# Two feed-forward layers on one core: the last activation in two halves, and stores of different batches untied

## The chip, the cores and the metric

The kernel runs on one core of one Trainium2 chip. The metric is device time in microseconds (us). Three runs of the kernel before took 1050.55, 1051.12 and 1052.24 us, median 1051.12 us. In names of engines, PE is TensorE, DVE is VectorE, ACT is ScalarE, POOL is GpSimd and SP is SyncE.

## The reference

The input x has 16 batches of 256 rows of 256 float32 values; cond_8 gives each batch 8 scores. Two layers follow each other, and each adds its result to x.

- Layer 0: each batch takes the one expert of 8 with its largest score. `hidden = silu(x Wup + bup) * (x Wgate + bgate)`, width 512; `x = x + hidden Wdown + bdown`.
- Layer 1: each batch takes its two best experts with weights w (a softmax of the scores, made to sum to 1), and in addition a shared expert that all batches use. Each expert is `(gelu(x Wgate) * (x Wup)) Wdown`, width 1024. The result is `x + sum of w * expert(x) + shared(x)`.

## The kernel before

**Units.** The work is cut into units. A `Pair` takes two batches that use the same expert and multiplies them as 2 x 2 blocks in Winograd's variant of Strassen's scheme, with 7 block products in place of 8 (`STEPS`, `Pair.up`, `Pair.down`). A `Single` takes one batch in the plain way. Layer 0 has 4 pairs and several singles; layer 1 has 12 routed pairs (`pairs`), 8 shared pairs (`shared`, the expert that all batches use) and singles for what is left over. Which batches form a pair is found on the chip, and a few variants ("arms") of the program's later parts are chosen by that.

**A pair's work.** The hidden width is cut into 4 quarters in layer 1 (2 in layer 0). For quarter j, PE does the seven steps `up(j, 0..6)`. For these POOL first makes four sums of the quarter's weights (`sums_q`, which calls `sums_a`: lines 479 to 482, tile s), except in the shared pairs behind the first, which load sums stored earlier. ACT copies PSUM results (line 522, tile cp), and DVE combines them with others into the four blocks C11, C21, C12, C22 of tile c (line 526): C11 after step 1, C22 after step 4, C21 after step 5, C12 after step 6. In layer 1, `act(j)` then takes gelu of the gate half of all four blocks on ACT (line 577, 128x1024) and multiplies by the other half on DVE (line 580, 128x1024) into blocks 0 to 3 of a tile of ring bt. `act_sums(j)` makes the three further sums on DVE (lines 472 to 474). When all quarters are there, `down(0..6)` multiplies with the down weights (line 597, four quarters in one step, so 8 matmul records), whose sums on POOL are `sums_d` (again lines 479 to 482, tile ds). `early` reads a first result out of PSUM (line 619 on ACT, or 612 on DVE in the last unit), and `late` finishes a block into tile ys (lines 626 and 630 on DVE).

**Order.** No scheduler orders the instructions: they are issued as the program is written. A small planner, `Line`, holds a clock: `line.main` runs a PE step and advances it, `line.later(n, f)` runs f once the clock is n further. `when_free(tag, f)` puts f off until a buffer of that ring has been given back (`give`). Engines and DMA queues each work in order, so an instruction that waits holds up all that stands behind it on its engine.

**Stores.** `done` puts a unit's `send` on a list, and the next `quarter` runs it. In layer 1 `send` issues on POOL one accumulating DMA per batch into `out` (line 451), so each batch's own row gains the unit's result. In layer 0 it issues on SP two plain DMAs per batch, to `x1d` (line 453) and to `out` (line 454). The row is an index held in a register, so the framework cannot know that two stores go to different rows: each waits until the one before it into the same tensor has landed. POOL's sums `s` and `ds` stand behind the stores on POOL; weight loads (line 409, 418) stand behind those of layer 0 on SP.

**The last unit**, `shared[-1]`, does not use `done`. It has loaded what `out` holds (`load_z`, line 515), adds it in `early`, and stores each finished quarter of the result from `late` (line 633): batch 0 on SP, batch 1 on ACT. Only here were stores of different batches declared independent, and only within the unit. Its last `act(3)` waits for a buffer of ring bt, which the unit before it, `shared[-2]`, gives back at its own `down(6)`.

Of the kernel before, what the change touches and what calls it, by code (L numbers as in the profile page):

```python
# [10 lines left out]
AF = mybir.ActivationFunctionType  # L11
ALU = mybir.AluOpType
# [3 lines left out]
B, S, D, E = 16, 256, 256, 8  # L16
# [39 lines left out]
UP, SINGLE_UP = 2, 8  # L56
# [3 lines left out]
def kernel(  # L60
# [10 lines left out]
    nc = tc.nc  # L71
# [9 lines left out]
    x1d = dram.tile([B, P, KD, S], F32, name="x1d")  # L81
# [30 lines left out]
    def take(tag, *shape, of=None):  # L112

        i = turns[tag].pop(0)
        if tag not in HELD:
            turns[tag].append(i)
        else:
            assert (tag, of) not in turns
            turns[tag, of] = i
        t = rings[tag][i]  # L120
        n = 1
        for d in shape:
            n *= d
        t = t[:, :n]
        if len(shape) == 1:
            return t
        names = "abcd"[: len(shape)]
        return t.rearrange(
            f"p ({' '.join(names)}) -> p {' '.join(names)}", **dict(zip(names, shape))
        )  # L130

    def when_free(tag, f):

        if turns[tag] and not turns["later", tag]:
            f()
        else:
            turns["later", tag].append(f)

    def give(tag, of):
        turns[tag].append(turns.pop((tag, of)))  # L140
        if turns["later", tag]:
            turns["later", tag].pop(0)()

    def bank(tag):
        return take(tag, N2)
# [210 lines left out]
    class Unit:  # L356
# [27 lines left out]
        def row(self, a, t, engine=SP):  # L384
            return a[bass.ds(self.batch(t, engine), 1)].rearrange("b p c s -> (b p) c s")
# [50 lines left out]
        def done(self, ys):  # L436

            line.results.append((self.layer, lambda: self.send(ys)))
            if self is shared[-2]:
                line.send()  # L440

        def send(self, ys):

            for t in range(self.width):
                b = self.batch(t, POOL if self.layer else SP)

                def row(a):
                    return a[bass.ds(b, 1)].rearrange("b p c s -> (b p) c s")

                if self.layer:  # L450
                    nc.gpsimd.dma_start(row(out), ys[:, :, t, :], accum_op=ALU.add)  # L451
                else:
                    nc.sync.dma_start(row(x1d), ys[:, :, t, :])
                    nc.sync.dma_start(row(out), ys[:, :, t, :])
            if self.layer or self.width == 2:
                give("ys", self)

    class Pair(Unit):
# [114 lines left out]
        def act(self, j):  # L573
# [6 lines left out]
            nc.vector.tensor_tensor(t[:, 0:4, :], u, v, ALU.mult)  # L580
            self.acts.append(t)

        def act_sums(self, j):
            t = self.acts[j]
            self.sums_b(t, t[:, 2, :])

        def down(self, k):

            tag, a, b = STEPS[k]
            if k == 0:  # L590
                self.ys = take("ys", KD, 2, S, of=self)
            if OPENS[k]:
                self.banks[tag] = bank({"X": "A", "Q": "B", "Y": "Y"}[tag])
            src = self.d[:, A_AT[a]] if a in A_AT else self.ds[:, S_AT[a]]
            d = self.banks[tag][:, :S]
            for j in range(self.kp):
                nc.tensor.matmul(  # L597
                    d,
                    lhsT=src[:, j, :],
                    rhs=self.acts[j][:, B_AT[b], :],  # L600
                    start=OPENS[k] and j == 0,
                    stop=j == self.kp - 1,
                    skip_group_check=True,
                )

            def early(block):
                c, t = block % 2, block // 2
                e = take("dz", S, of=(self, block))
                self.copies[block] = e
                src = self.banks["X"][:, :S]  # L610
                if self.last:
                    nc.vector.tensor_tensor(e, self.z[:, c, t, :], src, ALU.add)
                elif not self.layer:
                    nc.vector.scalar_tensor_tensor(  # L614
                        e, src, self.bd[:, c : c + 1], self.xt[:, block, :], ALU.add, ALU.add
                    )
                else:
                    w = 1.0 if self.at is None else self.weight(t)
                    nc.scalar.activation(e, src, AF.Copy, scale=w)

            def late(block, tag, sign):
                c, t = block % 2, block // 2
                e, src = self.copies[block], self.banks[tag][:, :S]
                dst = self.ys[:, c, t, :]
                if self.layer and self.at is not None:
                    nc.vector.scalar_tensor_tensor(  # L626
                        dst, src, self.weight(t, sign), e, ALU.mult, ALU.add
                    )
                else:
                    nc.vector.tensor_tensor(dst, e, src, ALU.add if sign > 0 else ALU.subtract)  # L630
                if self.last:
                    queue = (nc.sync, nc.scalar)[t]
                    store = queue.dma_start(self.out[t][:, c, :], dst)
                    for other in self.stores[1 - t]:
                        tc.declare_no_dep(store.ins, other.ins, reason="another batch")
                    self.stores[t].append(store)
                give("dz", (self, block))

            if k == 0:
                early(C11)  # L640
            elif k == 1:
                late(C11, "Y", 1)
            elif k == 2:
                early(C12)
            elif k == 4:
                early(C22)
                early(C21)
                late(C22, "Q", -1)
            elif k == 5:
                late(C21, "Y", 1)  # L650
            elif k == 6:
                late(C12, "Q", -1)
                give("d", self)
                for j in range(self.kp):
                    give("bt", (self, j))
                if not self.layer:
                    give("bt", self)
                if not self.last:
                    self.done(self.ys)

        def run(self, line, among):

            self.start()
            for j in range(self.kp):
                line.quarter(self, j)
                for k in range(6):
                    line.main(UP, lambda j=j, k=k: self.up(j, k))

                line.later(2 * UP, lambda j=j: self.up(j, 6))
                if not self.layer:  # L670
                    line.later(UP + 1, lambda j=j: self.act0(j, 1))
                line.later(
                    3 * UP, lambda j=j: when_free("bt", lambda: self.act(j))
                )
                line.later(6 * UP, lambda j=j: self.act_sums(j))
                for f in among[j] if j < len(among) else ():
                    f()
            step = self.step or (6 if self.layer else 3)
            for k in range(7):
                line.later(self.first + step * k, lambda k=k: self.down(k))  # L680
# [106 lines left out]
    shared = [Pair(next(names), 1, None, (2 * i, 2 * i + 1)) for i in range(NPR)]  # L787
# [155 lines left out]
    line = Line()  # L943
# [55 lines left out]
    def follow(units, behind=True):  # L999
# [3 lines left out]
        if known == start + Q_AHEAD - 1:  # L1003
            u, j = quarters[known]
            u.load_q(j, behind=behind)

    run(units[0])
    for k in arms(0):

# [10 lines left out]
        for a, p in zip(places[4:], pieces):  # L1020
            a.append(p)
        follow([*mid, *units[1], *tails[1]], behind=False)
        run([*mid, *units[1]])
        while line.routed < len(steps):
            line.route()
        for k in arms(1):
            left = ones[2 * k :]
            rest = [*tails[1], *left[:-1], *more_pairs[:k], *shared[1 - NB :]]
            turns["xs"], turns["d"] = [0, 1], [*turns["d"], 2]
            for u in rest:  # L1030
                among[u] = [[] for _ in range(u.kp)]
            if left:

                host = rest[len(left)]
                for j in range(host.kp):
                    among[host][j].append(partial(left[-1].piece, line, j, among=True))
                left[-1].po_bank, left[0].po_bank = "A", "B"
                shared[-NB].first = 24
            follow(rest)
            run(rest)  # L1040
            line.flush(1 << 30)
            line.send()
# [58 lines left out]
```

## Time and profile before

| what | value |
|---|---|
| three runs, median | 1051.12 us (1050.55 to 1052.24) |
| the profiled execution's own time | 1051.36 us |
| its span, first to last instruction | 1049.7 us |
| granted TensorE clock | 0.999 |
| PE busy | 1038.2 us (99%), 4750 matmul records |
| DVE busy | 777.0 us (74%) |
| POOL busy | 446.7 us (43%) |
| ACT busy | 371.3 us (35%) |
| stores of layer 1 on POOL, line 451 | 46, mean 1.065 us on POOL, 5.1 us to landing |

The profile gives for each engine how long it was busy, for groups of instructions the mean duration and what ended the idle time before them, and a chain of waits: from the last instruction back to what released it, and so on to the start. Times in the chain and in the timeline are microseconds from the span's start. A `x8` behind a PE entry counts matmul records: each matmul of 128x256 in float32 leaves two.

### The profile page before, as it was taken

The page shows a single profiled execution, that of the slowest core. Times are in us where ns is not written, and L with a number is a line of the kernel's source. Part 1 is how long each engine was busy: PE and PEld are TensorE (multiplying, and loading weights), DVE is VectorE, ACT ScalarE, POOL GpSimd, SP SyncE. Part 2 cuts the span into 40 slices and gives each one's busy share as a digit, 9 for nine tenths or more (in the row PEclk, how much of TensorE's full clock was granted, in tenths as well). Part 3 has the DMA queues.
Part 4 walks back from the last instruction along what each step waited for, and adds up shares of the span by engine and source line. Part 5 has one row for each costly group of instructions (what it writes and reads, how often), then busy time and mean ns, then how long its engine had stood idle before and what let it go on. Part 6 is the DMA issues. An engine that isn't in the chain of part 4 may idle for free.

```text
span 1049.7 us, 14152 instructions
## 1 busy us (share of the span) xinstructions
PE 1038.2 (99%) x4750; PEld 900.3 (86%) x4750; DVE 777.0 (74%) x1207; ACT 371.3 (35%) x583; POOL 446.7 (43%) x492
## 2 busy tenths in 40 slices
PE   9999999999999999999999999999999999999998
PEld 6778888888888888888888888888888888888886
DVE  7789978878687877887777778777766236776764
ACT  2444353535333333333333333333333123333331
POOL 2946331221043765666476556645201245630000
PEclk9999999999999999999999999999999999999999
DMA  7636656656664355345335533543655445356522
GB/s 237 241 127 203 240 181 194 207 166 236 200 235 119 88 140 140 93 109 140 98 87 138 140 98 103 140 122 83 178 159 171 133 136 156 91 180 184 183 75 45
DMA packets 60974, 157.47 MB, mean 150 GB/s; under 512 B 7506, under 2 KB 27090, under 8 KB 56658
## 3 DMA queue, kind: packets, MB, share of 16 engines
q1 hardware_dynamic: 47618, 140.90, 40.3%
q0 software_dynamic: 12976, 15.21, 9.4%
q8 instruction: 42, 0.69, 0.3%
q14 instruction: 50, 0.41, 0.1%
q10 hardware_dynamic: 288, 0.26, 0.1%
HBM read 132.23 MB, written 24.12 MB: 149 GB/s over the span
## 4 chain that ended last, share of the span: by engine, by line
PE 89%; DVE 7%; issue 2%; ACT 1%; DMA 1%; SPq 0%; DVEq 0%; ACTq 0%
PE X L541 24%; PE Q L541 16%; PE Y L541 16%; PE A L597 12%; PE B L597 9%; PE Y L597 8%; DVE c L526 2%; PE X L692 2%; PE Q L692 1%; DVE bt L580 1%; PE A L722 1%; DVE bt L472 1%; DVE bt L473 1%; PE B L722 1%; ACT c L577 1%
## 5 line engine op out<-in xcount | busy, mean ns | idle before, releaser
L522 ACT ACTIVATE cp<-X 128x512 f32<-128x512 f32 x318 | 189.5, 596 | 519.2 <-PE X L541 518.6
L580 DVE TENSOR_TENSOR bt<-c 128x1024 f32<-128x1024 f32 x106 | 145.7, 1374 | 102.8 <-ACT c L577 93.0
L541 PE MATMUL Y<-xt,q 128*128 128x256 f32 x736 | 189.8, 380 | 1.1 <-DVE c L526 0.6
L541 PE MATMUL Q<-xt,s 128*128 128x256 f32 x736 | 189.5, 380 | 0.6 <-DVE c L526 0.6
L541 PE MATMUL X<-xt,s 128*128 128x256 f32 x736 | 189.5, 380 | 0.0
L526 DVE TENSOR_TENSOR c<-cp,Q 128x512 f32<-128x512 f32 x212 | 144.3, 681 | 37.4 <-ACT cp L522 32.9
L526 DVE TENSOR_TENSOR c<-cp,Y 128x512 f32<-128x512 f32 x212 | 144.1, 680 | 22.4 <-PE Y L541 22.0
L541 PEld LDWEIGHTS Y<-xt,q 128*128 128x128 f32 x736 | 138.9, 190 | 23.2 <-DVE c L526 3.9
L451 POOL DMA_DIRECT2D out_dram<-ys x46 | 49.0, 1065 | 255.7 <-DVE ys L626 103.2
L541 PEld LDWEIGHTS Q<-xt,s 128*128 128x128 f32 x736 | 139.3, 190 | 21.2 <-DVE c L526 2.5
L541 PEld LDWEIGHTS X<-xt,s 128*128 128x128 f32 x736 | 139.3, 190 | 20.5 <-ACT cp L522 1.4
L479 POOL TENSOR_TENSOR s<-q 128x256 f32<-128x256 f32 x78 | 72.1, 924 | 131.8 <-PE Q L541 66.2
L482 POOL TENSOR_TENSOR s<-s,q 128x256 f32<-128x256 f32 x78 | 62.5, 801 | 101.0 <-PE Q L541 101.0
L597 PE MATMUL A<-bt,ds 128*128 128x256 f32 x424 | 101.5, 379 | 1.4 <-DVE dz L614 1.4
L597 PE MATMUL B<-bt,ds 128*128 128x256 f32 x424 | 101.4, 379 | 0.0
L577 ACT ACTIVATE c<-c 128x1024 f32<-128x1024 f32 x92 | 96.7, 1052 | 12.9 <-DVE c L526 12.7
L472 DVE TENSOR_TENSOR bt<-bt 128x512 f32<-128x512 f32 x113 | 95.0, 840 | 0.7 <-DMA bt<-x_dram 0.6
L541 PE MATMUL X<-xt,q 128*128 128x256 f32 x368 | 94.4, 379 | 0.0
L597 PEld LDWEIGHTS A<-bt,ds 128*128 128x128 f32 x424 | 80.4, 190 | 13.0 <-POOL s L481 1.4
L597 PEld LDWEIGHTS B<-bt,ds 128*128 128x128 f32 x424 | 80.5, 190 | 11.2 <-ACT ys L737 0.3
L597 PE MATMUL Y<-bt,d 128*128 128x256 f32 x376 | 90.0, 379 | 0.0
L597 PEld LDWEIGHTS Y<-bt,d 128*128 128x128 f32 x376 | 71.4, 190 | 9.7
(163 smaller groups left out, 1157.1 us busy)
## 6 DMA issues: line engine op xcount, KB each, us to landing
q<-wq_dram SPq DMA_DIRECT2D x114, 512.0 KB, 3.7
d<-wd_dram SPq DMA_DIRECT2D x22, 1024.0 KB, 6.6
s<-qsums SPq DMA_DIRECT2D x28, 512.0 KB, 4.9
xt<-x1d SPq DMA_DIRECT2D x46, 256.0 KB, 4.3
out_dram<-ys POOLq DMA_DIRECT2D x46, 256.0 KB, 5.1
ds<-dsums SPq DMA_DIRECT2D x7, 1024.0 KB, 6.3
d<-wd_dram SPq DMA_DIRECT2D x7, 513.0 KB, 5.1
bt<-x_dram SPq DMA_DIRECT2D x14, 256.0 KB, 4.7
```

The costliest lines, as they stand in the source:

```text
L451: nc.gpsimd.dma_start(row(out), ys[:, :, t, :], accum_op=ALU.add)
L472: tt(t[:, 4:6, :], t[:, 0:3:2, :], t[:, 2:4, :], ALU.subtract)
L479: tt(s("S1"), a("A21"), a("A22"), ALU.add)
L482: tt(s("nS4"), s("S2"), a("A12"), ALU.subtract)
L522: nc.scalar.activation(t, self.banks["X", j], AF.Copy)
L526: nc.vector.tensor_tensor(self.c[j][:, block].rearrange("p m s -> p (m s)"), self.copies[n, j], self.banks[tag, j], op,)
L541: nc.tensor.matmul(self.banks[tag, j][:, bass.ts(m, S)], lhsT=self.q[j][:, m, A_AT[a], :] if a in A_AT else self.s[j][:, m, S_AT[a], :], r ...
L577: nc.scalar.activation(u, u, AF.Gelu_apprx_tanh)
L580: nc.vector.tensor_tensor(t[:, 0:4, :], u, v, ALU.mult)
L597: nc.tensor.matmul(d, lhsT=src[:, j, :], rhs=self.acts[j][:, B_AT[b], :], start=OPENS[k] and j == 0, stop=j == self.kp - 1, skip_group_che ...
L692: nc.tensor.matmul(dst[:, bass.ts(half, S)], lhsT=self.q[j][:, m, 2 * half + c, :], rhs=self.xt[:, c, :], start=(c == 0), stop=(c == KD - 1),)
L722: nc.tensor.matmul(self.po[:, bass.ts(c, S)], lhsT=self.d[:, 2 * c + half, j, :], rhs=self.acts[j][:, bass.ts(half, S)], start=(j == 0 and ...
```

## The change

Three edits.

1. In the last unit's last quarter, `act` is replaced by `act_half`, called twice. It takes no buffer of ring bt but one of ring xt (the ring that holds the layer's x), and it takes the gelu and the product for blocks 0 and 1 (C11, C21) as soon as the clock allows behind step 5, and for blocks 2 and 3 (C12, C22) right behind step 6.
2. `send` keeps its stores in `self.sent`, and declares each of them independent of the unit's earlier stores into the same tensor. Stores of one unit are still ordered behind those of the units before it.
3. The last unit's stores are also declared independent of those of `shared[-2]`.

On PE the order of the instructions is the same in both kernels. On DVE, the last quarter's product (one instruction of 128x1024, which stood behind two `late` steps of `shared[-2]`) becomes two of 128x512 that stand ahead of these: one ahead of the combination that makes C12, one behind it. On ACT one gelu of 128x1024 becomes two of 128x512. On POOL and SP the order is the same, and waits for a DMA are dropped from the second store of each unit.

```diff
+        @staticmethod
+        def apart(store, others):
+            for other in others:
+                tc.declare_no_dep(store.ins, other.ins, reason="another batch")
+
         def send(self, ys):
 
+            self.sent = []
             for t in range(self.width):
...
                 if self.layer:
-                    nc.gpsimd.dma_start(row(out), ys[:, :, t, :], accum_op=ALU.add)
+                    store = nc.gpsimd.dma_start(row(out), ys[:, :, t, :], accum_op=ALU.add)
+                    self.apart(store, self.sent)
+                    self.sent.append(store)
                 else:
-                    nc.sync.dma_start(row(x1d), ys[:, :, t, :])
-                    nc.sync.dma_start(row(out), ys[:, :, t, :])
+                    store = nc.sync.dma_start(row(x1d), ys[:, :, t, :])
+                    self.apart(store, self.sent[::2])
+                    self.sent.append(store)
+                    store = nc.sync.dma_start(row(out), ys[:, :, t, :])
+                    self.apart(store, self.sent[1::2])
+                    self.sent.append(store)
...
+        def act_half(self, j, half):
+
+            if half == 0:
+
+                self.acts.append(take("xt", 7, S))
+            t, k = self.acts[j], slice(2 * half, 2 * half + 2)
+            u, v = self.c[j][:, k, 0, :], self.c[j][:, k, 1, :]
+            nc.scalar.activation(u, u, AF.Gelu_apprx_tanh)
+            nc.vector.tensor_tensor(t[:, k, :], u, v, ALU.mult)
...
                 if self.last:
                     queue = (nc.sync, nc.scalar)[t]
                     store = queue.dma_start(self.out[t][:, c, :], dst)
-                    for other in self.stores[1 - t]:
-                        tc.declare_no_dep(store.ins, other.ins, reason="another batch")
+                    self.apart(store, [*self.stores[1 - t], *shared[-2].sent])
                     self.stores[t].append(store)
...
-                for j in range(self.kp):
+                for j in range(self.kp - self.last):
                     give("bt", (self, j))
...
-                line.later(
-                    3 * UP, lambda j=j: when_free("bt", lambda: self.act(j))
-                )
+                if self.last and j == self.kp - 1:
+
+                    line.later(1, lambda: self.act_half(j, 0))
+                    line.later(2 * UP, lambda: self.act_half(j, 1))
+                else:
+                    line.later(3 * UP, lambda j=j: when_free("bt", lambda: self.act(j)))
```

## The prediction

> **What bounds the kernel now.** I read the page's busy shares first, then the chain of waits, then timelines where the chain leaves PE.
>
> ```profile
> PE 1038.2 (99%) x4750; PEld 900.3 (86%) x4750; DVE 777.0 (74%) x1207; ACT 371.3 (35%) x583; POOL 446.7 (43%) x492
> ```
>
> PE is the bound. In the chain, back-to-back PE rows run at 0.86 us per 4 records and 1.73 per 8, that is 0.216 us a record. So time can only come from the places where a PE row starts later than the row before it plus its records at 0.216. I took these from PE's timeline. From 17 us on they add up to about 12 us: some 5.3 up to 81 us (layer 0), 0.6 at 117, 0.8 from 130 to 247, 1.2 from 295 to 306, 0.7 at the singles from 838 to 889, and the rest, 3.3, in the two sorts of place that the change touches.
>
> The first is in the tail, in the chain:
>
> ```profile
> 1030.60 1.74 PE B L597 x8
> 1032.34 0.02 issue
> 1032.37 0.42 DVE ys L630
> 1032.79 1.15 DVE bt L580
> 1033.93 0.04 issue
> 1033.98 0.70 PE A L597 x2
> 1034.67 1.73 PE Y L597 x8
> ```
>
> The last unit's down(0) could have run from 1032.34 to 1034.07 (8 records, 1.73). Its last quarter came late: the product L580 stood behind a late step that waits for PE's row of 1030.60, so the row ended at 1034.67. Loss: 0.60 us. After it all is back to back to 1045.05.
>
> The second recurs in layer 1 after each routed pair's stores. POOL's timeline:
>
> ```profile
> 445.36 1.08 POOL L451 DMA_DIRECT2D out_dram<-ys  x1 [0.27 <-DVE c L526]
> 450.22 1.06 POOL L451 DMA_DIRECT2D out_dram<-ys  x1 [3.77 <-DVE c L526]
> 450.81 1.22 POOL L479 TENSOR_TENSOR s<-q 128x256 f32<-128x256 f32 x1
> 452.12 1.07 POOL L480 TENSOR_TENSOR s<-s,q 128x256 f32<-128x256 f32 x1
> 454.89 1.28 POOL L479 TENSOR_TENSOR ds<-d 128x512 f32<-128x512 f32 x1
> 457.47 2.25 POOL L481 TENSOR_TENSOR ds<-d 128x512 f32<-128x512 f32 x1
> ```
>
> and the chain over the same stretch:
>
> ```profile
> 449.26 1.29 DVE c L526 x2
> 450.54 2.07 DVE bt L472
> ...
> 454.27 1.28 DVE c L526 x2
> ...
> 455.57 1.06 ACT c L577
> ...
> 458.52 1.28 DVE c L526 x2
> 459.80 0.04 issue
> 459.84 1.13 PE Y L541 x4
> ```
>
> The second store starts 4.86 us after the first: that is the first one's landing (5.1 us median), not the DVE combination that the bracket names, which was long done. Then POOL has eight sums to make without a pause, up to 460.96, and DVE's SBUF instructions beside them stretch:
>
> ```profile
> L472 DVE TENSOR_TENSOR bt<-bt x113: 674/686/2254, 24.8 to 1034.0; 128x512 f32<-128x512 f32 x113
> ```
>
> L472 took 2.14 us here against a median of 0.686, L473 0.83 against 0.426, L474 0.85 against 0.426, L580 1.93 against 1.226: 1.45 + 0.40 + 0.42 + 0.70 = 3.0 us of stretch. PE's Y row starts at 459.84 where 458.73 + 0.86 = 459.59 was due, and the next row 0.11 later than its four records allow: 0.36 us lost.
>
> **The Trainium skill.** "SBUF — State Buffer", section "SBUF: two separate sides": DVE and GpSimd share a port pair under an exclusive lock, which a DVE instruction with two SBUF inputs takes against a GpSimd one that reads SBUF; the first holds it for its whole instruction. The trace agrees: L472, L473, L474 and L580 stretch, L526 beside them, with one operand in PSUM, stays at 0.68. "DMA: Bandwidth & Descriptors", section "SWDGE vs HWDGE vs iDMA": accumulating DMAs go through GpSimd, which writes their descriptors into SBUF; the trace has POOL busy 1.07 us for each. The same page, section "Anatomy of one DMA — SWDGE (gpsimd) path": the semaphore fires only when the last byte is confirmed, and the wait for it sits on the issuing sequencer; the 4.86 us on POOL are that. No page has a price for the half products; the trace has.
>
> **The change, part by part.**
>
> *Halved activation.* Removed from the path: L580's wait for the late step and for the bt buffer. Half 0's gelu: ACT takes 1.05 for 1024 columns and 0.60 for L522's 512, so I take 0.62 (between half, 0.53, and whole, 1.05). C21 is ready at 28.74 (all times here + 1000), gelu to 29.4; the product stands behind L474 (ends 30.27) and, at L472's size, takes 0.69: ends 30.9. C12 to 31.5, gelu to 32.15, second product to 32.85. PE needs this quarter at 32.34 + 6 x 0.216 = 33.64: 0.8 us spare, even if the whole tile is waited for. Both late steps stand behind it now: 32.85 + 0.42 + 0.42 = 33.7 against 32.79 before. Who waits: L472 to L474 (33.7 to 35.0, 33.96 to 35.56 before), L612 (to 35.4), which PE's third row, due at 35.80, waits for: 0.4 us spare. The Y and B banks that the late steps read are next written well after 33.7 (B at 37.5), and POOL's last stores, whose data come 2 us later at 33.3, are no longer waited for. So cost 0, gain 0.60; if the 0.4 is missed by as much again, 0.2 remains.
>
> *Second stores on POOL (46 stores, two to a pair).* The second goes out right behind the first, at 446.7 in place of 450.22. What follows on POOL is held by PE then: L479 needs step 3 of the older quarter (PE's Q row at 446.64, so 447.7), L482 step 6 (Q at 450.96, so 452.1). So three sums run 447.8 to 450.6, the fourth 452.1 to 452.9, and the ds sums 452.9 to about 458 in place of 454.89 to 460.96. DVE's L472 to L474 (450.46 on) then meet one sum's end and pay about 0.2 of their 2.27; L526 by 453.4, gelu by 454.5, L580 still meets a ds sum (1.93) and ends at 456.4; the next L526 then waits for ACT's copy at 457.1 and not for DVE. Against 458.52 that is 1.3 us early, four times the loss of 0.36. Beside this, the second store and L479 now meet L580 at 447.24: it pays up to 0.8, and DVE's idle 0.80 ahead of 449.26 covers that. Losses of this sort, each with its following row: 0.51 at 350, 0.18 at 387, 0.27 at 423, 0.36 at 460, 0.47 at 497, 0.08 at 570, 0.31 at 606, 0.47 at 751: 2.65 us; the other four routed pairs lose nothing. The pair at 518 is a trial made by the kernel itself: its second store came 0.64 us later relative to the first, its L580 met no sum (1.27), and PE lost nothing. I book three quarters, 2.0: the bounds are 2.65 and, since some sums meet L580 or L472 wherever they lie, 0 or a loss (rivals).
>
> *Second stores on SP (layer 0).* SP waited 17.0 us in 7 places for a landing. What is behind it: weight loads and, at 77.85, loads of x1d. All are made some quarters ahead, and no PE or DVE wait of after 70 us names a DMA, so this gives 0; if the cover fails it costs nothing either, the loads being earlier. Both stores in flight at once may land later than 5.1; the next that needs them is a unit later, some 36 us.
>
> *Last unit's stores.* C11's goes out near 36.9 rather than at 40.94; but the last, C12's, waits for data of 1045.49 and follows at once. 0.
>
> *Added instructions:* one on ACT, one on DVE, on engines idle 65% and 26%: 0.
>
> Sum: 0.60 + 2.0 = 2.6 off the profiled 1051.36 gives 1048.8; the median shown lies 0.24 below that run, so 1048.5 on its footing.
>
> **Rivals.**
> 1. *The collision only moves.* POOL has the same work, so another DVE instruction with no slack may stretch as much. For: the sums' total is unchanged. Against: slack of 0.8 ahead of 449.26 and 1.3 after. Tail alone: 1051.12 - 0.6 = 1050.5.
> 2. *The tail stays, the pairs gain.* L612 comes late, or the first rows of down wait for all of the last tile with a later product. Spare 0.4 and 0.8 speak against. 1051.12 - 2.0 = 1049.1.
> 3. *Slower.* The second store's 1.06 and L479's 1.22 both get the port ahead of L580, which ends at 446.7 + 1.06 + 1.22 + 1.22 = 450.2 rather than 448.46, 0.94 past the 449.26 that L526 needs. It decides against the change once the lateness at 449.26 is more than L472 to L474 get back (2.3). If they get back nothing, 8 pairs without slack lose 0.94 each, 7.5: with the tail's gain 1058. Against: L479 waits for PE until 447.7, so L580 is first.
>
> **Numbers.** Forecast (own range 1047.2 to 1049.2) 0.62; rival 1 0.22; rival 2 0.08; rival 3 0.08. All losses gone is 1051.12 - 3.25 = 1047.9; a run's spread widens that to 1047.0 at the low end. The high end takes in rival 1 and its spread, 1051.0, and leaves out rival 3. About 0.2%, 2.1 us, is what a measurement of this kernel can tell from no change; it lies at 1049.0, inside the forecast's upper end. Faster: 0.56 of the forecast's 0.62 and half of rival 2, 0.60. Slower: most of rival 3, 0.07. Same: 0.33.
>
> **What would show it.** Right: second stores about 1.3 us after the first; L472's maximum down from 2254 ns to near 1.4 us in the pairs; no late PE row at 350, 423, 460, 497, 606, 751; the tail's PE rows from 1030 to the end without a break, the last DVE instruction 0.6 us nearer to the row of 1030.60. Wrong: late PE rows in these pairs at other places; a DVE chain that ends in PE again after 447; L612 ahead of PE's third row of the tail.

## The result, and the profile after

| | before | changed |
|---|---|---|
| median on the same chip, 8 runs each | 1050.68 us (1049.51 to 1052.29) | 1047.39 us (1046.76 to 1047.79) |
| ratio, 95% interval | | 0.9967 [0.9958, 0.9976] |
| profiled execution, span | 1051.36, 1049.7 us | 1047.37, 1045.7 us |
| granted TensorE clock | 0.999 | 1.0 |

The change saves 3.3 us; 2.6 were forecast. The median of 1047.39 us lies near the fast end of the forecast range (1047.2 to 1049.2). Not only the median fell: the runs of the kernel before lie 2.8 us apart, those of the changed one 1.0.

Lines have moved: the store on POOL L451 is L457 now, the combination L526 is L538, the bt sums L472 to L474 are L484 to L486, the product L580 is L592, the half product is L603, the sums on POOL L479 to L482 are L491 to L494, `early` is L641 on ACT (L634 on DVE in the last unit), `late` is L648 and L652. The engines' busy shares, from the page of the changed kernel:

```profile
PE 1034.8 (99%) x4750; PEld 900.8 (86%) x4750; DVE 754.1 (72%) x1208; ACT 371.2 (35%) x584; POOL 444.6 (43%) x492
```

DVE has one instruction more than before and is busy 22.9 us less: stretch beside POOL has gone, not work.

**The tail.** The chain of waits of the changed kernel (start, duration, what):

```profile
1027.34 1.73 PE B L619 x8
1029.07 1.73 PE A L619 x8
1030.80 1.73 PE Y L619 x8
1032.52 1.73 PE A L619 x8
...
1039.43 1.74 PE B L619 x8
1041.17 0.02 issue
1041.19 0.42 DVE ys L652
```

The row of 1027.34 is the one that stood at 1030.60 before. The row behind it, the last unit's down(0), now begins where it ends; the 0.02, 0.42, 1.15 and 0.04 us of DVE and issue that stood between are gone. The last DVE instruction begins 13.85 us behind the row of 1027.34, against 14.47 behind that of 1030.60 before: 0.62 us nearer.

**A routed pair.** POOL's timeline of the changed kernel, at the pair that the prediction showed (idle time and its releaser in brackets):

```profile
443.80 1.08 POOL L457 DMA_DIRECT2D out_dram<-ys  x1 [0.29 <-DVE c L538]
446.05 1.06 POOL L457 DMA_DIRECT2D out_dram<-ys  x1 [1.16 <-DVE ys L648]
446.65 1.22 POOL L491 TENSOR_TENSOR s<-q 128x256 f32<-128x256 f32 x1
...
450.88 0.73 POOL L494 TENSOR_TENSOR s<-s,q 128x256 f32<-128x256 f32 x1 [1.49 <-PE Q L553]
451.57 1.27 POOL L491 TENSOR_TENSOR ds<-d 128x512 f32<-128x512 f32 x1
```

and DVE's, with the line of the bt sum over the whole kernel (shortest, median, longest in ns):

```profile
447.68 0.69 DVE L538 TENSOR_TENSOR c<-cp,Q 128x512 f32<-128x512 f32 x1 [0.80 <-ACT cp L534]
...
448.88 1.05 DVE L484 TENSOR_TENSOR bt<-bt 128x512 f32<-128x512 f32 x1
449.97 0.42 DVE L485 TENSOR_TENSOR bt<-bt 128x256 f32<-128x256 f32 x1
...
454.49 2.01 DVE L592 TENSOR_TENSOR bt<-c 128x1024 f32<-128x1024 f32 x1 [2.44 <-ACT c L589]
456.42 0.67 DVE L538 TENSOR_TENSOR c<-cp,Q 128x512 f32<-128x512 f32 x1
457.02 0.68 DVE L538 TENSOR_TENSOR c<-cp,Y 128x512 f32<-128x512 f32 x1
```

```profile
L484 DVE TENSOR_TENSOR bt<-bt x112: 674/685/1432, 24.4 to 1025.4; 128x512 f32<-128x512 f32 x112
```

```profile
457.15 1.03 PE L553 MATMUL X<-xt,q 128*128 128x256 f32 x4
458.01 1.03 PE L553 MATMUL Y<-xt,q 128*128 128x256 f32 x4
```

The second store no longer waits 3.77 us for a landing. The first sum behind it now lies ahead of the bt sum L484, which takes 1.05 us in place of 2.14. PE's Y row starts when it is due, 0.86 us behind the X row; before, it was 0.25 late. (A row is late when it starts later than the row before it plus that row's records at 0.216 us.) No PE row from 330 to 800 us is late any more. Pairs recur every 36.26 us (median distance of one pair's first store from the next one's); before, it was 36.28 to 36.69.

### The profile page after: what moved, and what is told of

It is laid out like the page before. It is cut to its first block, busy times and chain, and to the rows that moved or that the text cites. A ratio compares the mean times of both kernels' runs of the same rounds, so it can differ in the third digit from the quotient of the medians.

```text
span 1045.7 us, 14137 instructions
## 1 busy us (share of the span) xinstructions
PE 1034.8 (99%) x4750; PEld 900.8 (86%) x4750; DVE 754.1 (72%) x1208; ACT 371.2 (35%) x584; POOL 444.6 (43%) x492
## 4 chain that ended last, share of the span: by engine, by line
PE 92%; DVE 3%; POOL 2%; issue 1%; DMA 1%; SPq 0%; ACT 0%; POOLq 0%; DVEq 0%
PE X L553 25%; PE Q L553 17%; PE Y L553 16%; PE A L619 13%; PE B L619 9%; PE Y L619 9%; PE Q L716 1%; PE X L716 1%; POOL s L491 1%; PE A L746 1%; PE B L746 1%; DVE c L538 1%; POOL s L492 0%; DMA d<-wd_dram 0%; POOL s L494 0%
## 5 line engine op out<-in xcount | busy, mean ns | idle before, releaser
L592 DVE TENSOR_TENSOR bt<-c 128x1024 f32<-128x1024 f32 x105 | 144.7, 1378 | 123.1 <-ACT c L589 114.1
L538 DVE TENSOR_TENSOR c<-cp,Q 128x512 f32<-128x512 f32 x212 | 144.3, 680 | 37.1 <-ACT cp L534 32.5
L538 DVE TENSOR_TENSOR c<-cp,Y 128x512 f32<-128x512 f32 x212 | 144.0, 679 | 22.5 <-PE Y L553 22.1
L457 POOL DMA_DIRECT2D out_dram<-ys x46 | 49.1, 1074 | 205.1 <-DVE ys L648 128.2
L491 POOL TENSOR_TENSOR s<-q 128x256 f32<-128x256 f32 x78 | 66.0, 846 | 155.3 <-PE Q L553 87.1
L494 POOL TENSOR_TENSOR s<-s,q 128x256 f32<-128x256 f32 x78 | 64.8, 831 | 119.1 <-PE Q L553 119.1
L484 DVE TENSOR_TENSOR bt<-bt 128x512 f32<-128x512 f32 x112 | 87.1, 778 | 0.2 <-DMA bt<-x_dram 0.2
L492 POOL TENSOR_TENSOR s<-s,q 128x256 f32<-128x256 f32 x78 | 80.3, 1030 | 6.1
```

The lines of the kernel that those rows point to most:

```text
L457: store = nc.gpsimd.dma_start(row(out), ys[:, :, t, :], accum_op=ALU.add)
L484: tt(t[:, 4:6, :], t[:, 0:3:2, :], t[:, 2:4, :], ALU.subtract)
L491: tt(s("S1"), a("A21"), a("A22"), ALU.add)
L492: tt(s("S2"), s("S1"), a("A11"), ALU.subtract)
L494: tt(s("nS4"), s("S2"), a("A12"), ALU.subtract)
L538: nc.vector.tensor_tensor(self.c[j][:, block].rearrange("p m s -> p (m s)"), self.copies[n, j], self.banks[tag, j], op,)
```

## The experiments

All times are medians, with the ratio to the kernel before on the same chip; its own medians were 1050.55 us (beside e1 to e4), 1050.77 (e5 to e8), 1050.68 (e9 to e11) and 1051.30 (e12).

### The halves alone, and with the last unit's stores

Run e1 has `act_half` and no more: its stores wait as before.

```diff
+                if self.last and j == self.kp - 1:
+                    line.later(1, lambda: self.act_half(j, 0))
+                    line.later(2 * UP, lambda: self.act_half(j, 1))
```

> The last unit's halved activation alone; all stores wait as in the kernel before. Theory (the pairs' second stores carry 2.65 of the gain, the halves 0.6): 0.6 us faster than before, 1050.1; no break in PE's rows between the tail's B row and the end; the pairs' second stores still some 4.8 us after the first, L472's line still above 2 us at its slowest, late PE rows at the pairs as before. Rival (the gain is the tail's, since everything behind it starts earlier): 3.3 us faster, 1047.4.

Measured: 1053.86 us (1053.42 to 1054.93), 1.0032 [1.0019, 1.0044]: 3.3 us slower, a miss. PE's tail is without a break, as it should be, but the last DVE instruction stands 8.2 us ahead of the span's end, against 4.2 before. The timeline of POOL in this kernel (L457 store):

```profile
1033.74 1.08 POOL L457 DMA_DIRECT2D out_dram<-ys  x1 [33.37 <-DVE ys L649]
1038.54 1.07 POOL L457 DMA_DIRECT2D out_dram<-ys  x1 [3.71 <-DVE dz L631]
```

and of SP (L652 is the store of the last unit), with SP's waits (us in total, times, longest):

```profile
1043.11 5.29 SPq L652 DMA_DIRECT2D out_dram<-ys  x2
```

```profile
SPq L652 <- DMA out_dram<-ys: 38.6, 2, 34.3
```

The late steps of `shared[-2]` stand behind the halves now, so its first store goes out 2.9 us behind PE's row of 1030.87; before, 0.9 behind that of 1030.60. The second waits for the first's landing, SP's first store of the last unit waits for the second's (1043.11 against 1040.94 before), and SP's second for that one's. This row of waits had just ended in time before. Now it is 2 us late, and it sets the end.

Run e5 adds the third edit to this, and keeps the waits in the pairs:

```diff
-                    self.apart(store, self.stores[1 - t])
+                    self.apart(store, [*self.stores[1 - t], *shared[-2].sent])
```

> The halved activation and the last unit's stores independent of those of the unit before it; the second stores of all units wait as before. Theory (the halves alone were slower because the last unit's first store stood behind the second POOL store, which their later data moved from 1036 to 1038.5): the loss of 3.3 us is gone, and the tail's 0.6 us break too, so 0.6 us faster than before, 1049.9; SP's first store of the tail goes out about 1037, at its data. Rival (the halves themselves, one gelu and one product more, or the later late steps cost the time): still 2 to 3.3 us slower.

Measured: 1050.46 us (1049.43 to 1052.09), 0.9998 [0.999, 1.0007]; SP's first store goes out at 1035.19, and the loss of e1 is gone. The two edits belong together: the halves cost 3.3 us without the untied last stores (stores declared independent of those of `shared[-2]`), and nothing with them. PE's tail is unbroken, but the 0.6 us that this should gain doesn't show at this interval; the waits in the pairs are still there, and scatter.

### The second stores, on POOL and on SP

```diff
-                    nc.gpsimd.dma_start(row(out), ys[:, :, t, :], accum_op=ALU.add)
+                    store = nc.gpsimd.dma_start(row(out), ys[:, :, t, :], accum_op=ALU.add)
+                    self.apart(store, self.sent)
+                    self.sent.append(store)
```

> Only the second accumulating store of a layer 1 unit is declared independent of the first; activation, layer 0's stores and the last unit's stores as before. Theory: 2.65 us faster than before, 1048.0; second stores 2.2 us after the first (held by the late step that fills them), no late PE rows at the routed pairs, the tail's 0.6 us break is there as before. Rival (the gain is the tail's): 0 to 0.3 us. Beside that, if the spread of the runs of before comes from when the first store lands, the runs of this kernel lie within about 1 us, against 2.8 us.

Measured: 1048.63 us (1047.87 to 1048.95), 0.998 [0.9972, 0.9988]: 1.9 us faster. No PE row in the pairs is late; the 0.51 us ahead of the last unit's down(0) is still there. The fourteen runs lie within 1.1 us; the thirty-nine of the kernel before on that chip lie 2.85 apart.

Run e3 does the same for layer 0's plain stores alone (`self.apart(store, self.sent[::2])` for x1d, `[1::2]` for out), and e6 is the changed kernel without just this.

> Only the second batch's stores of layer 0 on SP are declared independent. Theory: 0 within 0.3 us, since nothing waits for what stands behind them. Rival: the late PE row at 117 us, which the changed kernel no longer has, is owed to them: 0.6 us faster, and the row at 117 is in time.

> The changed kernel with layer 0's stores on SP waiting for each other as before; all else changed. Theory: as the changed kernel, 3.2 to 3.3 us faster than before, 1047.3. Rival (the row at 117 us, late before and in time in the changed kernel, is owed to layer 0's stores together with the rest): 0.6 us less gain, 1047.9, with the row at 117 late.

Measured: e3 1050.50 us (1049.22 to 1051.62), 0.9999 [0.9991, 1.0008]; e6 1047.79 us (1047.46 to 1048.18), 0.9972 [0.996, 0.9983]. Layer 0's part is worth nothing on the kernel before, and at most 0.4 us on the changed one, which these intervals don't tell from 0. A row near 117 us, 0.5 late before, is in time in the changed kernel and late in e6, but also late in e3, which has the part, and in time in e5, which has not. It is in time in all six profiles of kernels that hold the whole change (the changed kernel and e8 to e12). What brings it in time stays open.

### Is it the wait, or what stands behind it?

In e4 all stores are declared as before. Only the second store of a routed pair is put behind the next sums on POOL, so that these no longer stand behind a landing:

```diff
+                if self.layer and t and self.routed():
+                    line.later(30, lambda: self.second(row(out), ys[:, :, 1, :]))
```

> The kernel before, with every wait kept; the second store of each routed pair stands later in POOL's order, behind the next unit's s and ds sums. Theory (it is the sums queued behind the wait that come too late and meet DVE's chain): as much as the second stores alone, 2 to 2.65 us faster than before, though the second store waits for the first one's landing. Rival (two stores in one another's way, or the landing itself, cost the time): no gain, within 0.3 us.

Measured: 1048.65 us (1047.98 to 1049.54), 0.9982 [0.9975, 0.999], 1.9 us: the whole of what e2 gains, though no declared order was taken away. Most of the pairs have no late row (0.14 at 350), and the bt sum (L481 in this kernel) is back to 0.69:

```profile
450.46 0.69 DVE L481 TENSOR_TENSOR bt<-bt 128x512 f32<-128x512 f32 x1
```

At its new place, 17 us behind the first store, the second finds the landing long past, so POOL is not held there either. What e4 shows is that the gain needs no two stores in flight, only the sums ahead of the wait. Whether POOL's wait costs by itself is told by the next runs.

In e7 these lines stand in `sums_q` and in `sums_d`: the routed pairs leave out both, so their quarters are multiplied with sums that are not theirs; stores and waits are those of before.

```diff
+            if self in pairs:
+                return
```

> The kernel before with POOL's sums s and ds of the routed pairs left out (those pairs multiply with what the tiles held, so their results are not the reference's); all waits of the stores are kept. Theory (DVE is late at the pairs because its two-input SBUF instructions meet POOL's sums, and the stores' wait only sets when): no late PE rows at the routed pairs, L580 in them at 1.23 us and not 1.9, about 2 us faster than before, 1048.5; L472 is stretched by at most the 1.06 of a store. Rival (the stores' own descriptors on POOL, or the landing, hold DVE): L472 as slow as before, above 2 us, and no gain.

Measured: 1047.60 us (1047.09 to 1048.20), 0.9969 [0.9958, 0.998]: 3.2 us faster, more than expected, since the sums' other collisions (rows at 117 and 304) go with them. The waits are still there, and cost nothing: ahead of the second store shown below POOL stands idle for 6.72 us, against 3.77 before. The run also answers what holds the bt sum. POOL's timeline of e7, and then DVE's (bt sums at L472 and L473):

```profile
447.71 1.07 POOL L451 DMA_DIRECT2D out_dram<-ys  x1 [6.72 <-DVE c L530]
```

```profile
447.93 0.69 DVE L472 TENSOR_TENSOR bt<-bt 128x512 f32<-128x512 f32 x1
448.65 0.42 DVE L473 TENSOR_TENSOR bt<-bt 128x256 f32<-128x256 f32 x1
```

L472 starts 0.22 us behind a second store and runs, all inside it, in its usual 0.69; the same at six more pairs of e7, 0.08 to 0.81 behind. In the kernel before, at the same distance (0.24, at 450.46), it took 2.14. The store doesn't hold it. What holds it is the sum right behind the store, which e7 leaves out.

### The dose: where the second store falls

The kernel before holds a trial of its own: the landing takes 4.7 to 5.5 us, from pair to pair. Set against each other, the second store's distance from the first and the time to the next pair (profiled execution of before, a pair a line):

```
pair at   second store   L472, us   to the next pair
408.84    4.76 behind    2.05       36.52
445.36    4.86           2.14       36.64
482.00    4.95           2.25       36.69
518.69    5.50           0.69       36.28
554.97    5.03           0.69       36.35
591.32    4.79           2.09       36.55
627.87    4.99           0.69       36.28
664.15    5.32           0.68       36.32
```

L472 starts 5.1 us behind the first store, whatever the second does. A store 0.13 us or more ahead of it brings the sum onto L472; one that is 0.10 ahead or less, or behind, doesn't. (In two pairs outside these eight, at 336 and 734, the second bt sum, L473, is held instead, for 1.77 and 2.56 us, and the rows at 350 and 751 are 0.41 and 0.36 late. So missing L472 isn't always enough.) To set the distance by hand, the changed kernel got n memsets on POOL, 128x128, between the two stores of the routed pairs:

```diff
                     self.sent.append(store)
+                    if t == 0 and self in pairs[:-1]:
+                        for _ in range(n):
+                            nc.gpsimd.memset(rw, 0.0)
```

> The changed kernel with 16 memsets of 128x128 on POOL between the two stores of each routed pair, which touch a tile that is no longer used; nothing waits for a DMA. They hold POOL[...], so that second store and sums start about as late as in the kernel before. Theory (the time at which the sums start decides): the late PE rows at the pairs come back, L472 at its slowest near 2 us, 1 to 2 us slower than the changed kernel. Rival (the wait for the landing, or the first store still in flight, cost the time): no slower than the changed kernel, within 0.3 us.

> As the run with 16 memsets, with 14. There the memsets took 0.288 us each and the second store began 5.96 us after the first, past DVE's L472, which begins 5.1 us after it. With 14 the second store should begin about 5.0 to 5.4 us behind the first; in the kernel before, the pairs with 4.69 to 4.98 us have L472 at 2 us and a late PE row, those from 4.99 us on have neither. Theory (what costs is that the store gets the port just ahead of L472, with the sums behind it): if the second stores begin under 5.0 us, L472 at 2 us, late PE rows and up to 2 us slower than the changed kernel; if over 5.0 us, neither, and no slower. Rival (the late rows of before came from the landing itself): no late rows at either offset.

> The changed kernel with 12 memsets (0.288 us each in the run with 16) on POOL between the two stores of each routed pair. Theory (what costs time is where the second store and the s sum behind it fall against the first bt product of the pair, not the landing as such): the second store starts about 5.45 - 2 x 0.288 = 4.9 us after the first, inside the 4.7 to 5.0 us at which the kernel before loses time, so that product takes about 2 us again (maximum 1.9 to 2.3 us) and late PE rows of 0.2 to 0.5 us come back at several pairs: 1048.4 to 1050.0, that is 1 to 2.6 us above the changed kernel. Rival (the wait for the landing itself is what cost, or the sums' order on POOL): no late rows at the pairs, that product below 1.5 us, 1047.4 like the changed kernel.

Measured:

```
memsets   second store   first bt sum, us   to the next pair   median, us
none      2.2 behind     1.0                36.26              1047.39
12        4.92           2.22 to 2.26       36.70              1050.99
14        5.44           0.68               36.26              1047.38
16        5.96           0.69               36.26              1047.43
```

Ratios: 0.9996 [0.9987, 1.0004] with 12, 0.9971 [0.996, 0.9981] with 14, 0.9967 [0.9956, 0.9979] with 16. My 16 were a miss: a memset took 0.29 us, 16 of them 4.6, and the store came behind the place where it hurts. With 12 it falls there. Eleven pairs have memsets, and eight of them lose 0.44 us each, 3.5 together. The median is 3.6 us above the changed kernel's, or 3.0 when each is set against the kernel before on its own chip. (In the pair at 444, L487 starts 0.3 us sooner and is not held; in the last two, at 734 and 770, the second store comes no later than in the changed kernel.) With 14 memsets POOL is held up for longer, and nothing is lost. This is the plainest evidence here against "POOL waits too long": 0.52 us more of delay takes the whole loss away.

POOL's timeline of the kernel with 12 memsets, pair at 480, and DVE's (L487 to L489 are the bt sums, L595 the product):

```profile
484.79 1.06 POOL L457 DMA_DIRECT2D out_dram<-ys  x1 [0.73 <-DVE c L541]
485.39 1.22 POOL L494 TENSOR_TENSOR s<-q 128x256 f32<-128x256 f32 x1
```

```profile
484.94 2.23 DVE L487 TENSOR_TENSOR bt<-bt 128x512 f32<-128x512 f32 x1
487.21 0.83 DVE L488 TENSOR_TENSOR bt<-bt 128x256 f32<-128x256 f32 x1
488.07 0.83 DVE L489 TENSOR_TENSOR bt<-bt 128x256 f32<-128x256 f32 x1
...
491.22 1.94 DVE L595 TENSOR_TENSOR bt<-c 128x1024 f32<-128x1024 f32 x1 [1.12 <-ACT c L592]
```

and its chain of waits behind that:

```profile
493.08 1.28 DVE c L541 x2
494.37 0.04 issue
494.41 1.13 PE Y L556 x4
```

The same pair with 14 memsets, POOL and then DVE:

```profile
484.99 1.06 POOL L457 DMA_DIRECT2D out_dram<-ys  x1 [0.73 <-DVE c L541]
485.58 1.22 POOL L494 TENSOR_TENSOR s<-q 128x256 f32<-128x256 f32 x1
```

```profile
484.62 0.68 DVE L487 TENSOR_TENSOR bt<-bt 128x512 f32<-128x512 f32 x1
485.34 1.76 DVE L488 TENSOR_TENSOR bt<-bt 128x256 f32<-128x256 f32 x1
487.13 0.84 DVE L489 TENSOR_TENSOR bt<-bt 128x256 f32<-128x256 f32 x1
...
490.29 1.27 DVE L595 TENSOR_TENSOR bt<-c 128x1024 f32<-128x1024 f32 x1 [1.12 <-ACT c L592]
```

Here the sum catches the second bt sum, L488. From L487's start to L489's end it is 3.96 us with 12 memsets and 3.35 with 14. These 0.6 us, and the product's 1.94 against 1.27 behind them, are the difference of a late row and one in time: the chain has slack, and the larger stretch uses it up. Where the first bt sum is held, in before, e1 and e12, the row at the pair's end is late by that sum's duration less 1.89 us, within 0.05: 0.17 for 2.05, 0.25 for 2.14, 0.36 for 2.25, 0.35 for 2.24 (the prediction's figures for these pairs count the following row's delay, about 0.1, as well).

### A version that may be a little faster, and the changed kernel again

Run e10 makes the down sums of layer 0 six steps later, so that the first of them don't meet the s sums that PE waits for:

```diff
-                self.later(12, u.sums_d)
+                self.later(18, u.sums_d)
```

> The changed kernel with layer 0's ds sums planned at 18 units behind their quarter in place of 12: on POOL the four ds sums of a pair change places with the four s sums behind them. In the changed kernel PE's rows at 44.18 and 51.65 us are 0.74 and 1.14 us late behind POOL's s sums, which stand behind the ds sums, and the row at 58.98, 1.21 late, waits for DVE. If POOL's order is what is late there, the row at 51 comes in time: about 1 us faster than the changed kernel, 1046.4. If the ds sums are then late themselves, or DVE is the next to be late, 0.

> The changed kernel again, on the chip of the two runs above, as what they are compared with: 1047.4, 3.3 us faster than before, no late rows at the routed pairs; the row at 117 us, in time in its first profile and late in six of ten profiles of all kernels, may be late here if that is chance.

Measured on one chip: e10 1046.85 us (1046.52 to 1047.33), 0.9967 [0.9955, 0.9979]; the changed kernel 1047.43 us (1047.22 to 1048.08), 0.9971 [0.9961, 0.9982]. All but one of the six runs of e10 lie below all eight of the changed kernel beside it, and the medians are 0.6 us apart; the two intervals overlap. The reason isn't confirmed. The row at 51 us is still 1.04 late (1.14 in the first profile of the changed kernel). The row at 44 is 0.35 late in place of 0.74, but 0.25 in e11's profile of the same changed kernel, where that at 51 is 1.48 late, so these two vary by themselves. What is shorter than in both profiles of the changed kernel is the lateness at 58 (0.54 against 1.21) and at 77 (0.36 against 0.56 and 0.57); a new late row, 0.22, stands at 106. Why those, wasn't tested.

## Why the prediction was right, point by point

**Halves: right to 0.2 us.** Put on the clock of before (3.26 us later, by the row of 1027.34), the products end at 1030.86 and 1032.84 (30.9 and 32.85 forecast), the late steps at 1033.5 (33.7), `early` at 1035.35 (35.4), ahead of the row of 1035.78. DVE's timeline of the changed kernel:

```profile
1026.92 0.68 DVE L603 TENSOR_TENSOR xt<-c 128x512 f32<-128x512 f32 x1
1027.52 0.68 DVE L538 TENSOR_TENSOR c<-cp,Q 128x512 f32<-128x512 f32 x1
1028.89 0.69 DVE L603 TENSOR_TENSOR xt<-c 128x512 f32<-128x512 f32 x1 [0.69 <-ACT c L602]
...
1031.68 0.41 DVE L634 TENSOR_TENSOR dz<-z,A 128x256 f32<-128x256 f32 x1
```

**The last unit's stores: booked at 0, and that failed as a price.** Against the kernel before it may be 0 (not tried alone); against the halves it is 3.4 us, as e1 and e5 show. The prediction said that POOL's last stores come 2 us later and "are no longer waited for", but not what that cover is worth if it is gone. Together the two edits gain 0.8 us by the medians of e2 and e6, 1.1 when each is set against its own kernel before: the break in PE's rows is 0.51 in e2's profiled execution, and the way from the last DVE instruction to the end is shorter as well, 4.09 us in e6 and in the changed kernel against 4.54 in e2 and 4.21 before.

**Second stores on POOL: the mechanism right, three of its terms not.**
- "Right behind the first, at 446.7": it comes 2.25 us behind and not 1.3, since its batch is filled by the late step L648, which waits for PE. That costs nothing.
- DVE's sums "pay about 0.2": they paid 0.36 (1.05 against 0.69). But the next combination is only 0.5 us earlier than before (456.42, on the clock of before 458.0, against 458.52), not 1.3. The working had gelu follow the combination at once. On ACT an `early` stands ahead of it and waits for PE's A row, which nothing moves. ACT's timeline of the changed kernel:

```profile
453.04 0.47 ACT L641 ACTIVATE dz<-A,wsort 128x256 f32<-128x256 f32 x1 [1.07 <-PE A L619]
453.41 1.05 ACT L589 ACTIVATE c<-c 128x1024 f32<-128x1024 f32 x1
```

The combination still ends at 457.70, 0.31 ahead of PE's Y row of 458.01; less stretch would have brought no more.
- "Three quarters, 2.0": all of the loss went. That 2.0 was still near the measured 1.9 is due to the other factor, the loss itself. The profiled execution of before held 2.65 us of it and took 1051.36, where the median is 1050.68. From the first store of the pair at 336 to that at 770 it took 434.4 us, the changed kernel 431.7; e1, e3 and e5, which have the same waits there, took 434.3, 433.4 and 433.6, so they lost 2.7, 1.7 and 1.9. How much depends on which landings fall in the window, run by run. Most of the wide scatter of before is this: it is down to 1.1 us in e2, where only these waits are gone.

**Layer 0's stores and the added instructions:** 0, within what the runs tell.

**The sum.** Pairs 1.9, halves with last stores 0.8 to 1.4 (e2 against e6 and the changed kernel, by the medians or each against its own kernel before): 2.7 to 3.3 of 3.3. The pairs' term came near its 2.0. So the 0.7 us that the forecast fell short lie in the tail, booked at 0.6, and in a rest (perhaps the row at 117). How they divide isn't settled: the intervals of the runs are each about 1 us to either side.

**The rivals.** "The collision only moves" fell: what is left of it lies on the next product, L592, which takes 2.01 us (1.93 before, as L580) but ends early enough that 0.31 us are to spare behind it. "The tail stays" fell with PE's unbroken rows. The slower rival had two parts wrong: L592 ahead of the stretch took its plain 1.22, and what it counted at "1.06 and 1.22" for store and sum is the sum's alone, by e7. Its idea, that a store at the wrong place costs more than a late one, is what 12 memsets show.

## What to carry to other kernels

Where a wait on POOL seems to cost time, ask which instruction is released at its end and what runs on DVE at that moment. Here the wait itself was free, and holding POOL still longer was as good as not holding it. When an edit reorders work so that a queue's last stores come later, price the waits behind these stores too: the halves were worth 0.6 us to PE and cost 3.3 us until the stores were untied.

## What the runs showed of the hardware

- **Which one gets the port isn't always told by the recorded starts.** The Trainium skill, "SBUF — State Buffer", section "SBUF: two separate sides", says that whichever of the two starts first gets the shared pair for its whole instruction, and the other is blocked. Blocked it is: with 12 memsets L487 ends 0.56 us behind the sum. But by the records L487 began first, at 484.94 against the sum's 485.39. In the kernel before and in e1, e3, e5 and e12, with a sum right behind a second store, the bt sum was held at every lead up to 0.48 us ahead of the sum, and ran in 0.69 from a lead of 0.50 on. Such a sum is recorded from 0.46 us before the store's end, and lasts 1.22 us where the same sum alone takes 0.73. Where POOL had stood idle before the sum, the records agree with the rule: in the changed kernel a bt sum 0.29 us ahead of the sum at 71.77 ran in its 0.69, and the sum took 0.98 for 0.72. Spans on POOL are rough, so I can't say whether the record or the rule is off behind a store; the measured border is what holds here.
- **A meeting can cost less than a whole instruction.** In the kernel before, the 128x256 sum L473 took 0.83 us for 0.42 beside a row of POOL's sums, where waiting for a whole one of these would add 0.73 to 1.2. It began in the middle of one (452.12 to 453.19) and ended 0.27 behind it, at 453.46; the trace doesn't tell a wait for the rest of that sum from a slower run.
- **A store's time on POOL doesn't hold DVE's two-input sums:** 0.69 beside the store of 1.07 us in e7. Nor do memsets: the product ran in 1.21 to 1.22 us beside a row of sixteen (e8), against 1.22 without.
